# Linear attention in one kernel with routed experts: chunks of 128 tokens become pairs of 64-token chunks

## The chip, the cores and the metric

The kernel runs on one core of a Trainium2 chip. The metric is the device time of one execution in microseconds (us); lower is better. Three executions of the kernel before gave 908.94, 910.54 and 915.1 us, median 910.54. A separate execution was profiled; the page shown later is of that one.

The engines of the core are TensorE (PE in the profile, its weight loads are PEld), VectorE (DVE), ScalarE (ACT), GpSimd (POOL) and SyncE (SP, which only issues DMAs here). TensorE multiplies a stationary operand with a moving one and writes to PSUM, eight banks of 512 fp32 words for each of 128 partitions. GpSimd does not read PSUM in this kernel.

## The reference, cut

Four sequences of 2048 tokens with 256 features. Attention is linear, with 16 heads of 16 features and a running state; then each token goes to two of eight experts.

```python
mod = (_silu(c) @ wmod).reshape(4, 6, 1, -1)       # sa, ca, ga, sb, cb, gb
h = layernorm(x) * (1 + ca) + sa
# attention, w_qkv and w_out, phi = elu + 1:
q, k, v = phi(h @ wq.T), phi(h @ wk.T), h @ wv.T    # per head
S_t = S_{t-1} + k_t v_t^T ;  z_t = z_{t-1} + k_t    # over the tokens of a sequence
out_t = (S_t^T q_t) / max(z_t . q_t, 1e-6)
x = x + ga * (out @ w_out.T)
# experts:
h = layernorm(x) * (1 + cb) + sb
gates = softmax(h @ w_router.T); the best two, capacity 1280 rows for each expert
hidden = silu(h @ w_gate.T)
y = sum over the kept experts e of gate_e * (hidden @ w_down[e].T)
x = x + gb * y
```

## The kernel before

**Tiling.** The 8192 tokens are 16 groups `g` of 512 (`G`), four groups for each sequence (`GPB`). A group has four steps `j` of 128 tokens (`P`). The main loop runs over the 64 steps `s` (and one more), and in each it works on several groups at once: attention of group `g`; projections (`project`, `values`, `keys_by_token`), running key sums and denominators (`running_keys`, `denominators`, `scaled_q`, `heads_apart`) of `nxt` = g+1; normalisation of g+2; second normalisation and router of `prv` = g-1; positions and row stores of `old` = g-2 and g-3. After the 64 steps the experts run over the rows that were stored by expert (`gate`, `down`); that stage is not touched by the change.

**Order.** The order on TensorE, ScalarE, VectorE and GpSimd is the order in which the program is written (`manual_schedule`); each engine runs its list in that order, and the framework only adds the waits. Two accesses to one PSUM bank of one tile are kept apart by a wait, also where they touch different columns.

**Attention of one step.** The 256 features lie on partitions in two halves `h`; within a half, four strips of 32 partitions `a` hold two heads each, and `qeo` holds the scaled queries once for the even and once for the odd heads (`q`).

- `scores` (L494): 8 products, 32 features x 128 keys against 2 x 128 queries, into the four banks `psc`, one for each strip. Then `at` (L500): two VectorE instructions of 128x1024 that multiply the scores by the triangle `tri`.
- `attend` (L570), one step later: 16 products, 128 keys x 32 value columns (`vpad`) against 128 columns of `at`, into `po`.
- `keep_state` (L514): 8 products of the keys by token (`kk`) with the values, into other columns of `po`.
- `take_out`: one ScalarE copy of `po` (`both`, L525), then two GpSimd instructions: `s_acc` adds the step's sum (L538), `s_msk` leaves the blocks of single heads (L540).
- `from_state` (L557): 8 products of the state before the step with the queries, into the next `po`. The state it uses (`s_old`) was made in the step before.
- `project_out` (L588): two products `pw`, then VectorE adds them to `x` (L589) and takes statistics (L325).

An fp32 product appears in the trace as two matmul records.

**PSUM.** Three banks rotate for everything called `bank(...)` (projections, transposes, `pd` of `denominators`, `pw`, the router's `pl`, `lt` and `pp`), four are `psc` (also `pr` of `scaled_q`), one is `po`.

**Around it.** In step 0 stand the query projections `pq` (L375) and `deviations`; in step 1 `positions(old)` (`pp`, L707), the values `pv` (L397) and `shift_rows(old)` (L618, VectorE, 128x1024); in step 2 `denominators`, `to_features`, `scaled_q` (L471) and `dispatch(old)` (L731 to L753, some fifteen small VectorE instructions, two of them `sel`, L751); in step 3 the key projections `pk` of g+2, the router's `logits` and `ranks(prv)` (L669 to L690). `scale_rows` (L612) is a GpSimd multiplication of 128x1024. `send` issues indirect DMAs on GpSimd (L770), eight for each group: three in step 3, three in the next step 1, two in step 2.

## Time and profile before

| | us |
|---|---|
| median of 3 executions | 910.54 |
| profiled execution | 915.75 |
| its span, first to last instruction | 913.8 |
| PE busy | 823.0 |
| DVE busy | 568.2 |
| POOL busy | 477.1 |
| ACT busy | 419.0 |
| mean granted TensorE clock | 0.960 |

| stretch of the span, us | PE busy | DVE busy | POOL busy | clock |
|---|---|---|---|---|
| 0 to 72, start | 58.80 | 40.39 | 19.73 | 1.00 |
| 437.6 to 470.7, one group | 30.67 | 28.95 | 23.23 | 1.00 |
| 548 to 608, last group's routing | 28.00 | 29.59 | 33.48 | 0.75 |
| 608 to 872, experts | 263.96 | 87.29 | 106.37 | 0.99 |

Busy time is the time in which at least one instruction of the engine runs. A row of the order in time gives start, duration, engine, line, operation, output and inputs, the number of instructions merged, and in brackets the idle time of the engine before it and what released it. Durations of matmul records overlap, and their ends are modelled; the distance from one row's start to the next one's is the better measure of what a stage costs. The chain of work that ended last is given as start, duration, engine, line.

### The profile page before, as it was taken

The page shows a single profiled execution, that of the slowest core. Times are in us where ns is not written, and L with a number is a line of the kernel's source. Part 1 is how long each engine was busy: PE and PEld are TensorE (multiplying, and loading weights), DVE is VectorE, ACT ScalarE, POOL GpSimd, SP SyncE. Part 2 cuts the span into 40 slices and gives each one's busy share as a digit, 9 for nine tenths or more (in the row PEclk, how much of TensorE's full clock was granted, in tenths as well). Part 3 has the DMA queues.
Part 4 walks back from the last instruction along what each step waited for, and adds up shares of the span by engine and source line. Part 5 has one row for each costly group of instructions (what it writes and reads, how often), then busy time and mean ns, then how long its engine had stood idle before and what let it go on. Part 6 is the DMA issues. An engine that isn't in the chain of part 4 may idle for free.

```text
span 913.8 us, 20612 instructions
## 1 busy us (share of the span) xinstructions
PE 823.0 (90%) x8245; PEld 576.5 (63%) x8245; DVE 568.2 (62%) x1158; ACT 419.0 (46%) x972; POOL 477.1 (52%) x605
## 2 busy tenths in 40 slices
PE   6899979999999899999999976539999999999995
PEld 4477657567567567567667555326776767767764
DVE  3667768988888888888988886513333333333331
ACT  4557656656567567566566423212222222222220
POOL 2323446575586586576676586523443444434434
PEclk9999989999999999999999989659999999999998
DMA  8499851331442242432121111255665656545233
GB/s 307 135 358 347 188 110 72 124 136 66 129 136 68 105 136 69 120 111 77 61 76 55 49 49 39 66 200 134 148 138 106 134 112 145 110 100 112 35 34 41
DMA packets 75111, 108.25 MB, mean 118 GB/s; under 512 B 9578, under 2 KB 47218, under 8 KB 75016
## 3 DMA queue, kind: packets, MB, share of 16 engines
q1 hardware_dynamic: 47672, 68.91, 24.8%
q0 software_dynamic: 21760, 31.99, 16.3%
q10 hardware_dynamic: 5584, 6.04, 2.0%
q8 instruction: 65, 1.06, 0.5%
q14 instruction: 30, 0.25, 0.1%
HBM read 45.07 MB, written 74.69 MB: 131 GB/s over the span
## 4 chain that ended last, share of the span: by engine, by line
PE 66%; DVE 15%; issue 6%; POOL 5%; ACT 4%; DMA 2%; POOLq 0%; DVEq 0%; ACTq 0%; SPq 0%
PE ph L821 14%; PE pe L834 13%; PE pq L375 6%; PE pv L397 5%; PE psc L494 5%; PE pk L375 5%; PE po L570 5%; PE pw L588 4%; DVE at L500 3%; PE po L557 3%; DVE sel L751 2%; DVE qs L471 2%; POOL slots L770 2%; PE pte L810 2%; POOL out_dram L843 1%
## 5 line engine op out<-in xcount | busy, mean ns | idle before, releaser
L843 POOL DMA_INDIRECT out_dram<-y,tok x80 | 123.3, 1542 | 180.7 <-DVE y L839 126.2
L500 DVE TENSOR_TENSOR at<-psc,tri 128x1024 f32<-128x1024 f32 x128 | 150.1, 1214 | 29.2 <-PE psc L494 28.8
L770 POOL DMA_INDIRECT slots<-hrow,idx x128 | 129.4, 1011 | 52.5 <-issue 36.4
L821 PE MATMUL ph<-hTe,wg_sb 128*128 128x512 f32 (+1 forms) x384 | 153.5, 527 | 0.0
L834 PE MATMUL pe<-wd,hid 128*128 128x256 f32 x640 | 150.5, 379 | 0.0
L827 DVE SCALAR_TENSOR_TENSOR hid<-th,ph 128x512 f32<-128x512 f32 (+1 forms) x96 | 57.5, 599 | 146.3 <-ACT th L826 146.3
L834 PEld LDWEIGHTS pe<-wd,hid 128*128 128x128 f32 x640 | 121.6, 190 | 37.0 <-issue 23.0
L826 ACT ACTIVATE th<-ph 128x512 f32<-128x512 f32 (+1 forms) x96 | 50.5, 526 | 156.4 <-PE ph L821 156.4
L821 PEld LDWEIGHTS ph<-hTe,wg_sb 128*128 128x128 f32 x384 | 70.4, 193 | 39.0 <-issue 32.5
L375 PE MATMUL pk<-hTa,wqkv_sb 128*128 128x512 f32 x128 | 69.3, 671 | 22.6 <-DVE gates L671 22.6
L494 PE MATMUL psc<-qeo,k 32*128 32x256 f32 x1024 | 74.7, 405 | 2.4 <-DVE qs L471 1.0
L588 PE MATMUL pw<-wob,both 128*128 128x256 f32 x236 | 63.2, 391 | 7.8 <-ACT both L525 5.5
L570 PE MATMUL po<-at,vpad 128*32 128x128 f32 x2048 | 69.8, 278 | 0.0
L839 DVE SCALAR_TENSOR_TENSOR y<-pe,rows 128x256 f32<-128x256 f32 x80 | 38.7, 484 | 49.6 <-PE pe L834 49.6
L570 PEld LDWEIGHTS po<-at,vpad 128*32 128x32 f32 x2048 | 53.9, 111 | 17.1 <-issue 16.9
L375 PE MATMUL pq<-hTa,wqkv_sb 128*128 128x512 f32 x128 | 61.3, 604 | 0.0
L494 PEld LDWEIGHTS psc<-qeo,k 32*128 32x128 f32 x1024 | 47.8, 188 | 19.7 <-issue 13.3
L397 PE MATMUL pv<-wqkv_sb,hTa 128*128 128x256 f32 x256 | 59.2, 384 | 0.0
L588 PEld LDWEIGHTS pw<-wob,both 128*128 128x128 f32 x236 | 41.9, 192 | 25.1 <-issue 10.1
L813 ACT COPY hTe<-pte 128x512 f32<-128x512 f32 (+1 forms) x48 | 24.7, 514 | 70.8 <-PE pte L810 70.6
L375 PEld LDWEIGHTS pk<-hTa,wqkv_sb 128*128 128x128 f32 x128 | 23.5, 201 | 46.7 <-issue 44.9
L397 PEld LDWEIGHTS pv<-wqkv_sb,hTa 128*128 128x128 f32 x256 | 47.6, 190 | 6.5 <-issue 0.4
(166 smaller groups left out, 1348.3 us busy)
## 6 DMA issues: line engine op xcount, KB each, us to landing
slots<-free SPq DMA_DIRECT2D x80, 262.0 KB, 5.1
rows<-slots SPq DMA_DIRECT2D x16, 1048.0 KB, 6.1
x<-in_x_dram SPq DMA_DIRECT2D x16, 512.0 KB, 6.1
out_dram<-x SPq DMA_DIRECT2D x16, 512.0 KB, 2.9
hrow<-mod_d SPq DMA_DIRECT2D x48, 128.0 KB, 3.5
rows<-slots SPq DMA_DIRECT2D x8, 524.0 KB, 7.6
wd<-in_wdT_dram ACTq DMA_DIRECT2D x8, 512.0 KB, 4.6
slots<-hrow,idx POOLq DMA_INDIRECT x128, 2.9
```

The lines of the kernel that those rows point to most:

```text
L375: nc.tensor.matmul(pq, wqkv_sb[:, k, o + h * P : o + (h + 1) * P], hT[:, k, :], start=(k == 0), stop=(k == NH - 1))
L397: nc.tensor.matmul(pv[:, i * D : (i + 1) * D], hT[:, k, (j + i) * P : (j + i + 1) * P], wqkv_sb[:, k, 2 * D : 3 * D], start=(k == 0), stop ...
L494: nc.tensor.matmul(psc[:, a, h], kT[r : r + 32, h, cols], qeo[r : r + 32, h, :, cols], start=True, stop=True,)
L500: masked = nc.vector.tensor_tensor(at, psc[:, 2 * m : 2 * m + 2].rearrange("p i h q t -> p (i h q) t"), tri.unsqueeze(1).to_broadcast([P, ...
L570: nc.tensor.matmul(po[32 * a : 32 * a + 32, h * P : (h + 1) * P], vp[:, j, h * 4 + a, q : q + 2, :], att[a // 2][:, a % 2, h, q, :], start ...
L588: nc.tensor.matmul(pw[:, :D], oT[:, h, :], wob[:, h, :], start=(h == 0), stop=(h == NH - 1))
L770: row = nc.gpsimd.indirect_dma_start(out=slots[:, :], out_offset=bass.IndirectOffsetOnAxis(ap=idx[:, c, j : j + 1], axis=0), in_=hr[:, j0 ...
L821: nc.tensor.matmul(ph[:, :m], wg_sb[:, k, f * P : (f + 1) * P], hTs[b][:, k, :m], start=(k == 0), stop=(k == NH - 1),)
L826: nc.scalar.activation(th[:, :m], ph[:, :m], AF.Tanh, scale=0.5)
L827: nc.vector.scalar_tensor_tensor(hids[b][:, f, :m], th[:, :m], 1.0, ph[:, :m], ALU.add, ALU.mult)
L834: nc.tensor.matmul(pe[:, :D], hids[b][:, f, j * P : (j + 1) * P], wds[e][:, f, :], start=(f == 0), stop=(f == NF - 1),)
L843: put = nc.gpsimd.indirect_dma_start(out=out[:, :], out_offset=bass.IndirectOffsetOnAxis(ap=toks[b][:, j : j + 1], axis=0), in_=y, in_offs ...
```

## The change

Attention runs in chunks of 64 tokens (`C`), two chunks of one step side by side: the first on the lower half of the partitions or rows, the second on the upper half.

- `scores`: 16 products of 64 keys x 2 x 64 queries; the two chunks write the two halves of the partitions. Only the two diagonal 64x64 blocks of a step are computed, so the mask `at` is one instruction of 128x1024 with the triangle `tri_c`.
- `attend`: 32 products over 64 keys. `keep_state`: 16 products, a sum for each chunk.
- `take_out`: ScalarE copies the outcome (`oT`); VectorE masks the two sums out of PSUM (`new`); GpSimd adds them to the state one after the other (`st`).
- `from_state`: 16 products; the first chunk takes the state before the step, the second the state after the first chunk (`mid`), which is made in the same step.
- PSUM: two rotating banks instead of three, four of `psc`, two of `po`. `pw`, `lt` and `pd` now lie in free columns of `psc`; `pl` and `pp` in free columns of `po`.
- Order: `shift_rows(old)` moves from step 1 to step 0, `dispatch(old)` from step 2 to the end of step 1, `positions(old)` ahead of `take_out` of step 1, `logits` behind `keep_state`; the eight `send`s of a group are issued three in step 2, three in step 3 and two in the next step 1.

```diff
-    ps = ctx.enter_context(tc.tile_pool(name="ps", bufs=3, space=PSUM))
+    ps = ctx.enter_context(tc.tile_pool(name="ps", bufs=2, space=PSUM))
+    def score_banks(name):
+        G_["free"] = ps_sc.tile([P, 4, 512], F32, tag="psc", name=name)
+        return G_["free"]
...
+        for c in range(2):
+            nc.gpsimd.tensor_copy(tri_c[c * C : (c + 1) * C, :], tri[c * C : (c + 1) * C, c * C : (c + 1) * C])
...
     def denominators(g):
-        pd = bank(f"pd_{g}")
+        pr = G_["pr", g] = score_banks(f"pr_{g}")
+        pd = pr[:, 1, 2 * P : 3 * P]
...
     def scores(g, j):
+        psc = score_banks(f"psc_{g}_{j}")
+        hq = psc[:, :, : NH * 2 * C].rearrange("p a (h q t) -> p a h q t", h=NH, q=2)
+        for h in range(NH):
+            for c in range(2):
+                cols = slice(j * P + c * C, j * P + (c + 1) * C)
+                for a in range(4):
+                    r = 32 * a
+                    nc.tensor.matmul(
+                        hq[c * C : (c + 1) * C, a, h], kT[r : r + 32, h, cols], qeo[r : r + 32, h, :, cols],
+                        start=True, stop=True,
+                    )
+        at = w4.tile([P, 4, NH * 2, C], F32, tag="at", name=f"at_{g}_{j}")
+        masked = nc.vector.tensor_tensor(
+            at,
+            psc[:, :, : NH * 2 * C].rearrange("p a (n t) -> p a n t", t=C),
+            tri_c.unsqueeze(1).unsqueeze(1).to_broadcast([P, 4, NH * 2, C]),
+            ALU.mult,
+        )
...
+    def keep_state(g, j, cs):
+        for h in range(NH):
             for a in range(4):
+                for c in cs:
+                    rows_ = slice(c * C, (c + 1) * C)
+                    o = NH * C + h * 32
+                    nc.tensor.matmul(
+                        po[32 * a : 32 * a + 32, c, o : o + 32],
+                        G_["kk", g][rows_, j, h, 32 * a : 32 * a + 32], vp[rows_, j, h * 4 + a, 0::2, :],
+                        start=True, stop=True,
+                    )
...
+    def take_out(last, g, j, cs):
+            oT = G_[("oT",) + last] = w2.tile([P, NH, 2, C], F32, tag="oT", name=f"oT_{g}_{j}")
+            nc.scalar.copy(
+                oT.rearrange("p h c t -> p c h t"), po[:, :, :o].rearrange("p c (h t) -> p c h t", t=C)
+            )
...
+        nc.vector.tensor_tensor(
+            new[:, :k].rearrange("p c (h q e) -> p c h q e", h=NH, q=2),
+            po[:, :k, o : o + n].rearrange("p c (h q e) -> p c h q e", h=NH, q=2),
+            bd.unsqueeze(1).unsqueeze(1).to_broadcast([P, k, NH, 2, DH]), ALU.mult,
+        )
+        if not first:
+            nc.gpsimd.tensor_tensor(st[:, 0], G_["state"], new[:, 0], ALU.add)
+        if k == 2:
+            nc.gpsimd.tensor_tensor(st[:, 1], st[:, 0], new[:, 1], ALU.add)
+        G_["mid"] = st[:, 0]
+        G_["next"] = st[:, 1]
...
     def from_state(g, j):
+        for h in range(NH):
+            for c in cs:
+                st = G_["state"] if c == 0 else G_["mid"]
+                for a in range(4):
...
+                        po[r, c, h * C : (h + 1) * C], st[r, h * 32 : (h + 1) * 32],
+                        G_["qs", g][r, h, j * P + c * C : j * P + (c + 1) * C],
+        G_["state"] = G_["next"]
...
     def attend(g, j):
+                    for c in range(2):
+                        rows_ = slice(c * C, (c + 1) * C)
+                        nc.tensor.matmul(
+                            po[32 * a : 32 * a + 32, c, h * C : (h + 1) * C],
+                            vp[rows_, j, h * 4 + a, q : q + 2, :],
+                            att[rows_, a, h, q, :],
...
     def project_out(g, j):
-        pw = bank(f"pw_{g}_{j}")
+        pw = G_["free"][:, 0, 2 * P :]
...
-        pl = bank(f"pl_{g}_{j0}")
+        pl = G_["po"][:, 0, O_SMALL : O_SMALL + P] if beside else bank(f"pl_{g}_{j0}")
-        lt = G_["lt", part] = bank(f"lt_{g}_{j0}")
+        lt = G_["lt", part] = G_["free"][:, 1, 2 * P : 3 * P]
-        pp = bank(f"pp_{g}_{j0}")
+        pp = G_["po"][:, 0, O_SMALL : O_SMALL + P] if beside else bank(f"pp_{g}_{j0}")
...
+            keep_state(g, j, cs)
+            if prv is not None and j == (2 if early else 3):
+                logits(prv, beside=True)
+            if old is not None and j == 1:
+                positions(old, beside=True)
+            take_out(last, g, j, cs)
...
-            if old is not None and j == 3 and not early:
-                send(old, 0, 3)
+            if old is not None and j in (2, 3) and not early:
+                send(old, 3 * (j - 2), 3 * (j - 1))
...
             elif j == 0:
                     running_keys(nxt, (0,))
+                if old is not None:
+                    shift_rows(old)
             elif j == 1:
                 done()
-                if old is not None:
-                    positions(old)
                     running_keys(nxt, (1,))
                 if g >= 3:
-                    send((g - 3, 0, NT), 3, 6)
+                    send((g - 3, 0, NT), 6, 8)
...
-                if old is not None:
-                    shift_rows(old)
+                if old is not None:
                     dispatch(old)
             elif j == 2:
-                if g >= 3:
-                    send((g - 3, 0, NT), 6, 8)
...
-                elif old is not None:
-                    dispatch(old)
```

## The prediction

> **What bounds the kernel now.** I read the page's busy times first, then the busy time by stage, then the chain of work that ended last, and last the order in time of TensorE and VectorE inside one steady group. A group is 512 tokens in four steps of 128; a step is called step 0 to step 3.
>
> ```profile
> PE 823.0 (90%) x8245; PEld 576.5 (63%) x8245; DVE 568.2 (62%) x1158; ACT 419.0 (46%) x972; POOL 477.1 (52%) x605
> ```
>
> ```profile
> 370.00:404.60 34.60, 32.54 (x447) 22.32 (x446) 28.93 (x58) 21.66 (x54) 22.12 (x32) 0.95 0.31 98
> 404.60:437.60 33.00, 31.00 (x432) 21.63 (x430) 28.81 (x58) 21.77 (x54) 21.42 (x30) 1.00 0.27 92
> ```
>
> These two rows are two groups: time, then busy PE, PEld, DVE, ACT, POOL, then the granted clock. TensorE is busy 31.0 of 33.0 us and VectorE 28.8, so neither has room; the share of 62% on the page hides that, because VectorE idles through the expert stage (608 to 872 us), which the change does not touch. Four of the eleven groups between 133.6 and 503.8 us have the clock 0.95 and about 34.6 us, the others about 33.0; the mean is 33.65.
>
> The chain gives what attention costs TensorE in one step:
>
> ```profile
> 409.32 0.57 PE po L557 x16
> 409.89 1.07 PE psc L494 x16
> 410.96 1.01 PE po L570 x32
> 411.98 0.12 PE po L514 x16
> 412.10 1.91 PE pq L375 x4
> ```
>
> From state, scores, attend, keep state: 2.78 us, with two records to each product. A record of 512 columns alone takes 430 ns (the second projection half, 1.72 us for 4), so one of 256 would take 215; scores' 16 would take 3.4 us in a row and take 1.07, four rounds of four. So products on separate parts of the array overlap, over three-fold where four parts are in use, in all three shapes that the trace has.
>
> Where the group waits is seen in time, TensorE first, then VectorE and GpSimd:
>
> ```profile
> 420.24 1.03 PE L588 MATMUL pw<-wob,both 128*128 128x256 f32 x4
> 421.46 3.70 PE L397 MATMUL pv<-wqkv_sb,hTa 128*128 128x256 f32 x16
> 425.66 1.15 PE L494 MATMUL psc<-qeo,k 32*128 32x256 f32 x16
> 432.93 1.15 PE L494 MATMUL psc<-qeo,k 32*128 32x256 f32 x16
> 440.37 1.96 PE L375 MATMUL pk<-hTa,wqkv_sb 128*128 128x512 f32 x4 [1.96 <-DVE gates L671]
> 442.83 1.15 PE L494 MATMUL psc<-qeo,k 32*128 32x256 f32 x16
> ```
>
> ```profile
> 417.75 0.69 DVE L384 SCALAR_TENSOR_TENSOR q<-exq,q 128x512 f32<-128x512 f32 x1 [0.77 <-ACT q L380]
> 418.36 1.22 DVE L433 TENSOR_TENSOR_SCAN zc<-ones_g,k 128x512 f32<-128x512 f32 x1
> 419.49 2.33 DVE L500 TENSOR_TENSOR at<-psc,tri 128x1024 f32<-128x1024 f32 x2
> 424.22 1.27 DVE L618 TENSOR_TENSOR hrow<-hrow,modr 128x1024 f32<-128x1024 f32 x1
> 435.02 2.02 DVE L751 SCALAR_TENSOR_TENSOR sel<-rank,slot 128x32 f32<-128x32 f32 x1
> 437.56 2.35 DVE L500 TENSOR_TENSOR at<-psc,tri 128x1024 f32<-128x1024 f32 x2
> ```
>
> ```profile
> 434.63 2.36 POOL L612 TENSOR_TENSOR hrow<-hrow,modr 128x1024 f32<-128x1024 f32 x1
> ```
>
> The one long wait of TensorE is in step 3: `dispatch` keeps VectorE until 437.5, so the mask (scores were done at 434.0), the routing and with it a free bank for `pk` come late, 1.96 us. Inside `dispatch`, `sel` takes 2.02 instead of 0.18 because GpSimd's `scale_rows` holds it off until 436.99. In step 1 TensorE does not wait at all: `pw` at 420.24 runs in a bank of its own while VectorE is still on the mask.
>
> **The change, part by part.** I count from O = 416.52, where the second query projection is issued and step 0's state products start; the next such point is 449.53, 33.0 us on.
>
> *Products.* Records per step go from 16+16+32+16 = 80 to 32+32+64+32 = 160, with half the columns each (keep state: the same 32 columns, half the rows). From state uses the same four parts of the array twice, so it stays at 0.57. Scores and attend can now use eight parts. Slow end, by the attend row at today's overlap: 64 records at half of 28 ns are 0.9, scores 1.07, keep state 0.24, drains as now: 2.9 us. Fast end, eight side by side: scores 0.65 (half of the 0.86 of its four rounds, and 0.2 of filling and switching), attend 0.45, keep state 32 at the 7.5 ns of its row, 0.24, with a drain 0.8 together: 2.02 us. I take the fast end, since the trace shows overlap to follow the number of separate parts; 0.75 us per step then leave TensorE.
>
> A page of the Trainium skill speaks against it: "TensorE: Matmul & The Clock Gate", section "Wait — 56ns, not 53.3ns?", has matmuls start no less than about 25 ns apart, which would make 160 records an estimated 4.0 us a step. Here the 16 records in 0.12 us are 7.5 ns apart, so the row decides. The same page, "Measured speedup vs the span model", reports 10.6-fold overlap for sixteen tiles; no row here shows more than four parts at once.
>
> *Mask.* L500 falls from two instructions of 1.21 to one; one new product of 128x128 from PSUM (`new`) is priced by `den` L451, 128x128 from PSUM, 0.28. VectorE: 4 x (1.21 - 0.28) = 3.7 us less of its 28.8. ScalarE's copy loses 64 columns (0.42 to 0.37, the 256-column row) and GpSimd keeps two additions of about 0.32. None of these sits on the path by itself.
>
> *Banks.* `pw`, `lt` and `pd` now lie in the banks of the scores, behind the same step's mask: TensorE must wait for `at` before `pw`, for `gates` before step 3's `pw`, and the next scores must wait for VectorE's `x` addition. This is where the time is decided. `pp` and `pl` go into the outcome bank and only put a 0.19 copy ahead of another on ScalarE. With two banks left for the rest, each projection needs the evacuation two before it; the ScalarE copies stand 1 us or more ahead at every such place (`kk` by O+5.1, `pv` at O+6.4), so nothing; without that cover it is up to 0.75, one copy.
>
> *Moves.* `shift_rows` (1.27) goes from behind step 1's work to step 0, directly ahead of step 1's mask. `dispatch` goes from step 2 to step 1, ahead of step 2's mask. GpSimd's eight row stores per group (each 0.98 and 0.30 of gap) are issued a step earlier, 3, 3, 2; `scale_rows` stands behind three of them instead of two, 1.3 us later, and its user is now in the next step 0, over 10 us on. SP's queue is passed by nothing.
>
> *State.* The second half of from state needs the sum of the same step: keep state, ScalarE copy 0.37, `new` 0.28, GpSimd 0.32 (1.24 where VectorE holds it off, 423.17). In step 1 it stands behind `rstd` 1.68 and `qs` 1.27 and is ready by O+7.9 to 8.8; TensorE comes at O+9.9. Covered; if not, each microsecond late is 12 over the kernel.
>
> **The path of a group, summed.** Step 1: `q` ends at O+1.92 as now, scan O+3.06, `shift_rows` O+4.3, the mask O+5.5. TensorE reaches `pw` at about O+3.4 and waits 2.1 us. Then `pw` 0.86, `pv` 3.54, from state 0.57: step 2's scores at O+10.5 (now 9.14). VectorE meanwhile: `x` and its statistics to O+7.3, scan (1.22 to 1.77) O+8.6 to 9.1, `dispatch`: 432.70 to 437.65 is 4.95, without the blocked 1.84 it is 3.1, and GpSimd's `qs` now beside it can block up to 1.1. Ends at O+11.7 to 13.3; mask O+12.9 to 14.5. `pd` waits for it. Then `pd` 0.55, transposes 1.02, `pw` 0.86, `x` 0.5, `pr` 0.75 (its bank waits for `x`), transposes 1.02, state 0.6 and handovers: 5.4 us to step 3's scores, O+18.3 to 19.9 (now 16.4). Step 3: scores, attend, keep 1.45, `pl` 0.46, `pk` 1.96, `lt` 0.11; then routing 3.7 (439.82 to 443.5) and `x` 0.41 with handovers before the next scores: 8.25 (now 9.9; the wait for `dispatch` is gone, the wait for `x` behind the routing is new). Step 0: 6.0 (now 6.70). Together 32.6 to 34.2 us, middle 33.35, against 33.0. The 3 us that leave TensorE come back as waits of 2.1, about 1.9, 0.6 and 0.9.
>
> *Clock.* Four groups of eleven, with one idle stretch of some 1.9 us each, lost 1.6 to a half-speed spell. Two such stretches per group make 2 x 4/11 x 1.6 = 1.15 on average (0.58 now). The same page, section "HAM oscillation — how this bites in real kernels", asks only for idle gaps under about 3.4 us; by it these stretches are free and a group costs 33.35. The rows show 1.9 to be enough, so they decide.
>
> So a group takes 34.5 instead of 33.65, and twelve of them (2 to 13) cost +10.2. Groups 0 and 1, without `dispatch`, gain 3 us of products and lose them to the same waits: +0.5. From 510 us on, two masks stand on the chain (529.74, 547.74) and are 1.1 shorter each, with some handovers: -3. Sum +7.7 on the profiled execution of 915.75 us (span 913.8, 2 around it). That execution lies above the median of 910.54, so the forecast is 910.5 + 7.7 = **918 us**, its own range 907 to 929 from the ends of the path (-9, +10 over twelve groups).
>
> **Rivals.** *Eight parts do not overlap more than four* (slow end): 0.87 us more in steps 3 and 0, +21, less some 3 because shorter waits slow the clock less often: 936. For it: no row shows more than four. Against: overlap followed the parts in every shape.
>
> *The masks are ready in time* (the other side). If `qs` does not block `dispatch`, the scan stays at 1.22 and the clock spells stay as they are, a group is 32.6 + 0.58, -0.47: -5.6 - 2.5 makes 902; without any spell 896. It decides where step 2's mask ends before O+12.9. For it: VectorE has 3.7 us less to do. Against: the order puts `shift_rows` and `dispatch` directly ahead of the masks that TensorE now needs.
>
> *Records cost their issue, not their columns.* If 28 ns of the attend row stay at 64 columns, a step is some 4.2 us, 4.3 more per group than the forecast: 970. The 7.5 ns row speaks against it. That the change does less than it says I put at nothing: the program has the 160 records and the one mask per step.
>
> **How the numbers follow.** Forecast 0.57, four parts 0.14, masks in time 0.25, issue 0.04. A measurement here tells about 1% from no change, 9 us. Faster than 901.4 needs the second rival with fewer spells, or the forecast's path shorter than its ends: 0.19. Slower than 919.6: nearly half of the forecast's range and two rivals: 0.48. Between: 0.33. The range goes from 899, the second rival with fewer spells, to 938, the first.
>
> **What would show it.** Right: `at` x64, 1.2 us; scores to keep state in 2.0 us a step; TensorE idle before `pw` of step 1 for 2 us, released by the mask, and before `pd`; no wait of `pk` for `gates`; clock under 1.00 in most groups. Wrong: step 1's `pw` not waiting, or the four product stages at 2.8 us or above, or a group under 33 us.

## The result, and the profile after

The changed kernel takes 978.18 us (median of 4; 976.95 to 983.78) against 911.87 us for the kernel before: 1.0738 times as long, 95% interval 1.068 to 1.0796. Forecast were 918 us and a range up to 938. The profiled execution took 979.24 us, its span 977.5, against 913.8 before.

The page's busy times and its instruction queue (packets, MB, share), then the busy time by stage for two steady groups (time; busy PE, PEld, DVE, ACT, POOL; clock, DMA share, GB/s):

```profile
PE 820.3 (84%) x13365; PEld 578.4 (59%) x13365; DVE 497.5 (51%) x1158; ACT 410.3 (42%) x971; POOL 471.8 (48%) x611
...
q8 instruction: 105, 1.72, 0.7%
```

```profile
433.91:471.03 37.12, 31.24 (x767) 21.82 (x765) 24.06 (x56) 21.06 (x53) 22.05 (x32) 0.95 0.23 73
471.03:508.04 37.01, 30.55 (x735) 21.62 (x733) 24.11 (x56) 21.05 (x53) 23.71 (x32) 0.97 0.25 78
```

VectorE has lost 4.7 us of work a group (28.8 to 24.1; forecast was 3.7). But a group takes 37 us instead of 33.0 to 34.6. TensorE's records have gone from 8245 to 13365, and the queue that brings instructions from 65 packets to 105.

The order in time of TensorE, in the group that begins at O = 427.46:

```profile
427.46 0.65 PE L578 MATMUL po<-qs,st 32*32 32x64 f32 x32
428.04 0.69 PE L510 MATMUL psc<-qeo,k 32*64 32x128 f32 x32
428.66 0.80 PE L594 MATMUL po<-at,vpad 64*32 64x64 f32 x60
...
432.97 1.10 PE L611 MATMUL psc<-wob,oT 128*128 128x256 f32 x4 [1.72 <-DVE at L515]
...
441.26 0.64 PE L460 MATMUL pr<-qs,hpick 128*32 128x128 f32 x16 [1.23 <-DVE at L515]
...
456.83 0.70 PE L510 MATMUL psc<-qeo,k 32*64 32x128 f32 x32 [1.88 <-DVE x L612]
...
458.55 3.58 PE L388 MATMUL pq<-hTa,wqkv_sb 128*128 128x512 f32 x4
```

The products are short, and the two waits for the mask are there, ahead of `pw` (432.97) and of `pd` (441.26, printed under the name of its bank, `pr`). New is a third wait, 1.88 us ahead of step 0's scores. Behind it the next projection takes 3.58 us instead of 1.9: the granted clock there is 0.50. VectorE and ScalarE show where it comes from:

```profile
451.22 0.19 DVE L694 TENSOR_TENSOR gates<-psc,mx 128x32 f32<-128x32 f32 x1
453.33 0.19 DVE L697 TENSOR_REDUCE sm<-gates 128x4 f32<-128x32 f32 x1 [1.93 <-ACT gates L695]
```

```profile
450.88 0.60 ACT L392 ACTIVATE exk<-pk 128x512 f32<-128x512 f32 x1
451.38 0.59 ACT L393 ACTIVATE k<-pk 128x512 f32<-128x512 f32 x1
451.85 1.33 ACT L498 ACTIVATE qeo<-qs,par 128x512 f32<-128x512 f32 x2
453.08 0.22 ACT L695 ACTIVATE gates<-gates 128x32 f32<-128x32 f32 x1
```

The router's exponent (L695) could run at 451.4, when VectorE has its argument. It stands on ScalarE behind an evacuation and `heads_apart` and runs at 453.08. The order on ScalarE is that of the kernel before; there `dispatch` made the argument late, and ScalarE had been idle for 0.49 us when it came:

```profile
440.26 0.23 ACT L672 ACTIVATE gates<-gates 128x32 f32<-128x32 f32 x1 [0.49 <-DVE gates L671]
```

The second new thing is a kind of idle time that the trace puts down to nothing it shows ("issue"):

```profile
99.48 0.25 PE L532 MATMUL po<-vpad,kk 64*32 64x32 f32 x4 [2.19 <-issue]
129.30 0.59 PE L611 MATMUL psc<-wob,oT 128*128 128x256 f32 x1 [5.58 <-issue]
302.30 1.02 PE L388 MATMUL pk<-hTa,wqkv_sb 128*128 128x512 f32 x2 [2.56 <-issue]
```

Thirteen such stops sum to 22.4 us; the kernel before has one, 3.6 us at 122.5. Its row, and its instruction queue on the page:

```profile
122.51 1.72 PE L361 MATMUL pta<-ident,xna 128*128 128x128 f32 x7 [3.63 <-issue]
...
q8 instruction: 65, 1.06, 0.5%
```

I numbered TensorE's instructions in the trace (weight loads, matmuls, semaphore events) in order of their start: the first instruction behind each of the thirteen, and behind the one before the change, has the same number, 193, modulo 256. The changed kernel's 105 packets carry 1.72 MB, 16.4 KB each. So these are the places where TensorE's own program comes in blocks of 256 instructions, and the 5120 added records, two instructions each, are the 40 added blocks.

Where 63.7 us of span went, from the start of `values` of one group to that of another:

| stretch (before / after, us) | before | after | difference | stops in it |
|---|---|---|---|---|
| start to 81.1 / 84.0 | 81.1 | 84.0 | +2.9 | 0 / 0.9 |
| two groups, DMA engines 0.86 / 0.80 busy in the first | 69.3 | 86.6 | +17.3 | 3.6 / 11.3 |
| eleven groups, to 522.2 / 580.8 | 371.8 | 410.2 | +38.4 | 0 / 8.4 |
| last routing, to 608.9 / 672.2 | 86.7 | 91.4 | +4.7 | 0 / 1.8 |
| experts, to the end | 304.9 | 305.3 | +0.4 | |

### The profile page after: what moved, and what is told of

Same layout as the page of the kernel before. It is cut to its first block, busy times and chain, and to the rows that moved or that the text cites. A ratio compares the mean times of both kernels' runs of the same rounds, so it can differ in the third digit from the quotient of the medians.

```text
span 977.5 us, 30896 instructions
## 1 busy us (share of the span) xinstructions
PE 820.3 (84%) x13365; PEld 578.4 (59%) x13365; DVE 497.5 (51%) x1158; ACT 410.3 (42%) x971; POOL 471.8 (48%) x611
## 3 DMA queue, kind: packets, MB, share of 16 engines
q8 instruction: 105, 1.72, 0.7%
## 4 chain that ended last, share of the span: by engine, by line
PE 64%; DVE 12%; ACT 9%; issue 8%; POOL 3%; DMA 2%; POOLq 0%; DVEq 0%; ACTq 0%; SPq 0%
PE ph L844 13%; PE pe L857 12%; PE pq L388 6%; PE pk L388 6%; PE psc L611 5%; DVE at L515 3%; PE po L594 3%; PE psc L510 3%; PE pv L410 3%; ACT xna L322 2%; PE pte L833 2%; PE pta L374 2%; PE ptm L374 2%; DVE zc L446 1%; PE po L578 1%
## 5 line engine op out<-in xcount | busy, mean ns | idle before, releaser
L611 PE MATMUL psc<-wob,oT 128*128 128x256 f32 x196 | 57.5, 418 | 43.4 <-DVE at L515 22.7
L515 DVE TENSOR_TENSOR at<-psc,tri_c 128x1024 f32<-128x1024 f32 x64 | 78.0, 1218 | 25.7 <-PE psc L510 25.5
L611 PEld LDWEIGHTS psc<-wob,oT 128*128 128x128 f32 x196 | 37.0, 203 | 58.7 <-issue 26.9
L388 PE MATMUL pq<-hTa,wqkv_sb 128*128 128x512 f32 x128 | 69.2, 670 | 0.0
L510 PE MATMUL psc<-qeo,k 32*64 32x128 f32 x2048 | 45.5, 283 | 26.0 <-ACT xna L295 14.8
L559 POOL TENSOR_TENSOR st<-st,new 128x64 f32<-128x64 f32 x60 | 28.8, 480 | 74.1 <-DVE new L553 73.9
L410 PEld LDWEIGHTS pv<-wqkv_sb,hTa 128*128 128x128 f32 x256 | 53.0, 207 | 14.8 <-issue 6.2
L594 PE MATMUL po<-at,vpad 64*32 64x64 f32 x4096 | 57.5, 232 | 0.9 <-issue 0.9
L418 ACT COPY vpad<-pv 128x256 f32<-128x256 f32 x64 | 20.7, 375 | 82.5 <-PE pv L410 82.5
L836 ACT COPY hTe<-pte 128x512 f32<-128x512 f32 (+1 forms) x48 | 24.7, 514 | 71.1 <-PE pte L833 71.0
L594 PEld LDWEIGHTS po<-at,vpad 64*32 64x32 f32 x4096 | 46.2, 108 | 12.6 <-issue 12.4
```

The lines of the kernel that those rows point to most:

```text
L388: nc.tensor.matmul(pq, wqkv_sb[:, k, o + h * P : o + (h + 1) * P], hT[:, k, :], start=(k == 0), stop=(k == NH - 1))
L410: nc.tensor.matmul(pv[:, i * D : (i + 1) * D], hT[:, k, (j + i) * P : (j + i + 1) * P], wqkv_sb[:, k, 2 * D : 3 * D], start=(k == 0), stop ...
L510: nc.tensor.matmul(hq[c * C : (c + 1) * C, a, h], kT[r : r + 32, h, cols], qeo[r : r + 32, h, :, cols], start=True, stop=True,)
L515: masked = nc.vector.tensor_tensor(at, psc[:, :, : NH * 2 * C].rearrange("p a (n t) -> p a n t", t=C), tri_c.unsqueeze(1).unsqueeze(1).to_ ...
L594: nc.tensor.matmul(po[32 * a : 32 * a + 32, c, h * C : (h + 1) * C], vp[rows_, j, h * 4 + a, q : q + 2, :], att[rows_, a, h, q, :], start= ...
L611: nc.tensor.matmul(pw, oT[:, h].rearrange("p c t -> p (c t)"), wob[:, h, :], start=(h == 0), stop=(h == NH - 1))
```

## Experiments

The runs fell on several chips of two kinds: on one kind the kernel before takes 911 to 914 us, on the other 956 to 963 us. Every ratio is against the kernel before on the same chip. What the expectations call the first and the second chip are these two kinds.

**The exponent first, and the moves undone.** `exp_first` issues the router's transposition, maximum and exponent ahead of `heads_apart` and the key projection; `order_back` leaves the changed order on ScalarE and puts `shift_rows`, `dispatch` and the row stores back where they were.

```diff
# exp_first, step 3
+                if prv is not None and not early:
+                    weights(prv)      # lt, mx, gates: the first half of ranks
                 heads_apart(nxt, (0,))
                 project(nrm, "k", 0, D, 2, later=True)
                 heads_apart(nxt, (1,))
-                logits_by_token(prv)
                 ranks(prv)
# order_back
-  step 0: shift_rows(old)   step 1: dispatch(old)   send 3, 3, 2 in steps 2, 3, 1
+  step 1: shift_rows(old)   step 2: dispatch(old)   send 3, 3, 2 in steps 3, 1, 2
```

> The changed kernel with the routing's transposition, maximum and exponent (lt, mx, gates) ahead of heads_apart and the first key projection in step 3, the rest of the routing where it was. Theory A: in the changed kernel VectorE waits 1.93 us for the exponent (453.33 behind ScalarE's exk, k and qeo), and TensorE then 1.87 us for x before step 0's scores. With the exponent before them the routing ends 2 to 3 us earlier, that last wait goes, and with it the half-clock spell that follows: 1.9 to 2.5 us for each of eleven groups, 950 to 958 us. Rival B (the bound is VectorE's and TensorE's work in that step, not the order on ScalarE): the wait moves to the earlier lt, nothing or under 6 us: 972 to 980 us.

> The changed kernel with the moves undone: shift_rows back in step 1, dispatch back in step 2, the row stores back at three in step 3, three in step 1, two in step 2. Theory A (the loss sits in three places: TensorE's own instruction stream stops at block boundaries, 22.5 us against 3.6; the routing's exponent in step 3 stands on ScalarE behind an evacuation, some 2 us a group; half-clock spells): the moves are not the cause. Step 1's pw then waits 1.2 us less (shift_rows 1.20 gone from ahead of the mask) and pd some 1.2 less, but dispatch (3.1 to 5 us) comes back ahead of step 3's mask and of the routing, so that step 3 gets longer by 2 to 4 us: between 975 and 995 us. Rival B (the moves put VectorE work ahead of the masks that TensorE now needs, and that is the loss): 1.7 and 1.2 us of waits go, with their spells, some 4 us a group on twelve groups: 930 us or less.

`exp_first`: 946.59 us, 1.0424 (1.0348 to 1.0499); again on another chip 948.7, 1.0363. That is 31.6 us less than the changed kernel, more than expected. The two steadiest groups, then TensorE around the place of the third wait, then VectorE:

```profile
378.61:411.77 33.16, 29.33 (x766) 21.16 (x765) 24.18 (x56) 20.93 (x53) 21.92 (x32) 1.00 0.32 106
411.77:444.88 33.11, 29.32 (x767) 21.15 (x766) 24.12 (x56) 20.94 (x53) 21.87 (x32) 1.00 0.25 82
```

```profile
427.18 0.33 PE L676 MATMUL psc<-ident,lgT 128*128 128x128 f32 x1 [0.39 <-ACT lgT L668]
...
432.32 0.69 PE L510 MATMUL psc<-qeo,k 32*64 32x128 f32 x32
...
433.99 1.99 PE L388 MATMUL pq<-hTa,wqkv_sb 128*128 128x512 f32 x4
```

```profile
428.34 0.19 DVE L711 TENSOR_REDUCE sm<-gates 128x4 f32<-128x32 f32 x1 [0.29 <-ACT gates L695]
```

The exponent takes 0.29 us out of VectorE's chain instead of 1.93, the scores of step 0 wait for nothing, and the projection runs at full clock. In the changed kernel the twelve waits there were 22.3 us and those of step 3's `pw` 7.4; `lt`, now early, gives 5.4 back. The rest of the gain, some 7 us, fits the clock, but no run shows it apart: ten of eleven groups were below 1.00, here seven, and the mean clock of the execution was 0.940, here 0.952. Against the kernel before, the profiled execution is still 27.8 us longer, 14.4 of them in the two early groups and 9.2 in the eleven; its stops at blocks are 24.7 us instead of 3.6, so most of what is left may be stops.

`order_back`: 963.06 us, 1.057 (1.0508 to 1.0632): between the two expectations, both missed. With `dispatch` in step 2 VectorE comes late to the router (`lt` waits 1.87 us for the mask) and its wait for the exponent is 0.29 us. So the moves did what they were to do, and in doing it laid bare the order on ScalarE. A third thing is needed: in the kernel before with the same moves (`before_moved` below) VectorE waits as long for the exponent,

```profile
440.26 0.18 DVE L674 TENSOR_REDUCE sm<-gates 128x4 f32<-128x32 f32 x1 [1.93 <-ACT gates L672]
```

and step 0's scores (440.96) wait for nothing, because `pw` has a bank of its own there and the scores need not wait for `x`. The moves, the order on ScalarE and `pw` in the scores' banks make the third wait together.

**Records or time.** Two versions of the kernel before with about the same added TensorE time, one in 80 records a step, one in four.

```diff
# more_records, keep_state
-        for h in range(NH):
+        for h in [h for _ in range(6) for h in range(NH)]:
# more_columns, end of keep_state
+        for _ in range(2):
+            nc.tensor.matmul(both[:, D + 64 : D + 256], G_["kk", g][:, j, 0, :], wqkv_sb[:, 0, :192], start=True, stop=True)
```

> The kernel before, with the products of keep_state issued six times over: 80 more matmul records in each of the 60 steps that keep the state, as many as the change adds, at 7.5 ns each 0.6 us a step, 36 us in all if TensorE's path takes all of it. Refill theory: each record is two instructions, so the program grows by 9600 instructions, 37 blocks of 256, and TensorE stops at some of the block boundaries as the changed kernel does: 910 + 36 + 8 to 19 us of stops, 954 to 966 us, and the trace shows stops named issue that sum to over 10 us. Rival (the stops of the changed kernel come from something else in it): 940 to 948 us, and stops of no more than some 4 us, as in the kernel before.

> The kernel before with two unused products of 128x192 columns added to each keep_state: four records a step of together about 0.64 us, the same busy time as the 80 small ones, but only 480 instructions in all. Both theories: 910 + up to 38, 940 to 950 us, with stops named issue of no more than some 4 us. Under the refill theory it is 8 to 19 us faster than the kernel with more records; under the rival the two differ by less than 5 us.

957.32 us, 1.05 (1.0446 to 1.0554), as the theory expected, against 937.97, 1.0286 (1.0233 to 1.034), 2 us under its range: 19.4 us between them. The page and the order in time of the first, and the one stop of the second:

```profile
q8 instruction: 102, 1.67, 0.7%
```

```profile
102.36 0.71 PE L464 MATMUL pr<-rden,spread 32*128 32x128 f32 x12 [3.24 <-issue]
110.20 0.80 PE L514 MATMUL po<-vpad,kk 128*32 128x32 f32 x70 [1.23 <-issue]
119.43 0.74 PE L570 MATMUL po<-at,vpad 128*32 128x128 f32 x18 [1.62 <-issue]
129.00 0.64 PE L557 MATMUL po<-qs,s_msk 32*32 32x128 f32 x16 [2.36 <-issue]
```

```profile
128.79 0.42 PE L574 MATMUL po<-at,vpad 128*32 128x128 f32 x8 [1.71 <-issue]
```

Nine stops, again all at number 193 of 256, 10.1 us against 1.7. The three early groups take 11.0 us more, the eleven groups behind them 7.5. Of those 7.5 only 1.1 are stops: the 96 small records take 1.33 us (425.13 to 426.46), the 16 with the two wide products 1.08, so the added work isn't quite equal, and only 8.4 of the 19.4 us are stops. So records alone bring stops at the blocks, about half of the changed kernel's; its other half needs more than their number.

`few_records` goes the other way: the kernel with the early exponent, attend and keep_state replaced by nine products with 18 records that don't compute their outcome.

```diff
# few_records
-        (64 records of attend)
+        for c, i in ((0, 0), (0, 1), (1, 0)):
+            nc.tensor.matmul(po[:, c, :P], G_["kk", g][:, j, c, :], att[:, 2 * c + i]..., ...)
-        (32 records of keep_state)
+        for c in cs * 3:
+            nc.tensor.matmul(po[:, c, o : o + 64], G_["kk", g][:, j, c, :], vp[:, j, :2, 0::2, :], ...)
```

> The kernel with the early exponent (1.036 to 1.042 times the kernel before, 24.7 to 27.1 us of stops at instruction blocks), with attend and keep_state left out and replaced by a few products of whole partitions that read the same tiles and keep the banks and the waits: three of 128x128 and six of 128x64, some 1.0 us a step as the 96 records had, but 18 records. The outcome of attention and the state are thereby not computed. 82 records a step, as many as the kernel before. Refill theory: the program is about 65 blocks long instead of 105, the stops fall to under 5 us and with them some of the half-clock spells that follow them: 1.010 to 1.022. Rival (the stops belong to the way these groups wait, or to the DMA load, not to the length of the program): stops of 15 us or more, 1.032 to 1.045.

66 packets, and one stop at a block, of 0.27 us, where the early exponent had 24.7 us of them. The three early groups, 122.2 us in a kernel with 105 blocks on a chip of the same kind (`spread_init` below), take 109.3. The time, 993.17 us, 1.0299, says nothing: the replacements took 2.2 us a step, not 1.0. So the stops follow the length of the program; what they are worth in all isn't measured by this run.

**The banks.** Waits taken out one by one from the kernel with the early exponent: `pw` in a rotating bank, then `pd` too, then `dispatch` at the end of step 3 (row stores three in step 0, three in step 1, two in step 2).

```diff
# pw_bank
-        pw = G_["free"][:, 0, 2 * P :]
+        pw = bank(f"pw_{g}_{j}")[:, :D]
# pw_pd_bank, late_dispatch: also
-        pd = pr[:, 1, 2 * P : 3 * P]
+        pd = bank(f"pd_{g}")[:, :P]
```

> The kernel with the early exponent (946.6 us, group 33.15 us), and pw of project_out back in one of the two rotating banks instead of the free columns of the scores' banks. Bank theory (what TensorE gained in products it waits for again, because pw sits behind the same step's mask): the 1.7 us wait ahead of step 1's pw goes; pv's second half then waits some 0.4 us for the x addition, and VectorE reaches dispatch 1.1 us earlier, so that the wait of pd stays at 1.2 to 1.5: a group of 31.8 to 32.2 us, 930 to 937 us. Rival (VectorE's chain of scan, shift_rows, mask, x and dispatch sets step 1 and 2, and the wait only changes its place to pd): a group of 32.9 to 33.2 us, 943 to 949 us.

> As the kernel before in this list, and pd of denominators in a rotating bank too. Bank theory: the wait of pd for step 2's mask (1.2 us) goes, but den still stands behind dispatch and that mask on VectorE, and the second transposition pta needs the bank that den frees: 0.3 to 0.6 us of wait stay there. A group of 31.0 to 31.5 us, 921 to 929 us. Rival (VectorE's chain sets it): no more than 3 us below the kernel with pw alone.

> As the kernel with pw and pd in rotating banks, and dispatch moved behind the key projections at the end of step 3, where the mask behind it has a whole step to spare; the row stores then go out three in the next step 0, three in step 1, two in step 2. If the order of VectorE's work was the rest of the loss, the waits of step 1 and 2 go to under 0.6 us each and step 0 stays free of waits: a group of 29.5 to 30.7 us, 905 to 918 us, near the kernel before in spite of 20 us of stops at instruction blocks. Rival (dispatch only displaces its wait to the next scores or to the query evacuation): a group of 31 us or more, 920 us or more.

On a chip of the second kind: 999.21 us (1.0365), 1002.89 (1.0388), 1041.6 (1.0804). The expected times were meant for the first kind, so only the ratios compare: none of the three gains came, and the rivals aren't contradicted. Two were repeated beside the early exponent on a chip of the first kind:

> The kernel with the early exponent once more, so that it stands beside the next two on one chip. On the first chip it took 1.042 times the time of the kernel before. Both theories: 1.035 to 1.05 times again.

> pw back in a rotating bank, once more, beside the kernel with the early exponent on one chip. On the second chip it took 1.0365 times the time of the kernel before, where 1.020 to 1.027 was expected. Bank theory: 1.0 to 1.5% under the kernel with the early exponent (the 1.7 us wait ahead of step 1's pw on twelve groups, less what comes back at pd and pv). Rival (the wait only changes its place): within 0.4% of it.

> pw and pd in rotating banks and dispatch at the end of step 3, once more on this chip. On the second chip it took 1.080 times the time of the kernel before, with 79 gaps of together 44 us inside small products, in the steps where its row stores are issued. Theory: without such gaps its groups take 29.5 to 31 us and it is 2 to 4% under the kernel with the early exponent; with them it is 3 to 5% over it. Rival (the order of dispatch itself is worse, through VectorE): 2% or more over it with no such gaps in the trace.

948.7 us (1.0363, 1.0304 to 1.0423), 968.08 (1.0611, 1.0546 to 1.0675) and 954.7 (1.0452, 1.0413 to 1.0491). `pw` in a rotating bank is 2% worse and `late_dispatch` 0.6%, outside all that was expected of either. The trace of TensorE with `pw` in a bank shows the wait moving:

```profile
441.52 0.64 PE L460 MATMUL pr<-qs,hpick 128*32 128x128 f32 x16 [1.95 <-DVE at L515]
442.10 1.40 PE L374 MATMUL pta<-ident,xna 128*128 128x128 f32 x8
443.62 2.08 PE L611 MATMUL pw<-wob,oT 128*128 128x256 f32 x4
...
460.17 1.88 PE L388 MATMUL pq<-hTa,wqkv_sb 128*128 128x512 f32 x4 [1.70 <-DVE new L553]
```

The 1.72 us ahead of `pw` are gone, but `pd` now waits 1.95 instead of 1.2 with a half-clock spell behind it (`pw` 2.08 instead of 1.03). The 1.70 us ahead of `pq` are something else: the profile names VectorE, but the weight load before it had started at 458.40, and `pq` has number 193 of 256, as at the same wait of the group before (1.93 us at 422.84). Both are stops at blocks, like the 3.18 us at 384.12; in the other groups nothing waits there. New in all groups is that the second halves of the projections wait 0.3 to 0.5 us for ScalarE. The eleven groups' clock is 0.95 instead of 0.97. `late_dispatch` has no wait of `pw` or `pd` for the mask and the clock at 0.99, but its steadiest groups take 33.4 to 33.9 us: with every small result in two rotating banks, five handovers of 0.24 to 0.66 us each stand on the path, and in most other groups step 2's `pw` waits 1.39 us for a copy (`hTa`). In these orders, with two banks for the rest, a wait that was taken out came back in other places.

`shift_early` keeps `pw` where it is, moves `shift_rows` to the start of step 0, where VectorE idles, and takes only `pd` out.

```diff
# shift_early, step 0
+                    shift_rows(old)
                 project(nxt, "q", 0, 0, 1)
 ...
-                    shift_rows(old)
```

> The kernel with the early exponent, with shift_rows at the beginning of step 0 (where VectorE idles some 2 us for the query's evacuation) instead of its end, and pd in a rotating bank, so that it doesn't wait for step 2's mask. If single waits can still be taken out while pw stays in the scores' bank: pw's wait in step 1 falls from 1.7 to 0.5 us and pd's from 1.2 to nothing, with some 0.7 back at the second transposition: a group of 31.5 to 32.2 us, 1.022 to 1.030. Rival (as with pw in a rotating bank, a wait that is taken out comes back at the next one on VectorE's chain, with a half-clock spell behind it): 1.036 to 1.050.

971.89 us, 1.008 (1.0052 to 1.0109), on a chip of the second kind: the best of the versions in chunks of 64 by its ratio, below what was expected. But the kernel before is itself slowed on that chip (below), so the ratio isn't to be set beside 1.036; beside `spread_init` (1.0298, below), the nearest run on the same kind, it is 2% lower. Its groups take 35.8 us there, not the 31.5 to 32.2 of the theory.

`spread_init` spreads the writes that fill the slots over twelve steps, for the stops:

> The kernel with the early exponent, with the 48 writes that fill the slots in steps 0 to 5 spread over steps 0 to 11, four instead of eight for each step. In that kernel the DMA engines are busy 0.95 to 1.00 from 50 to 130 us, and the stops at instruction blocks there sum to 10.8 of 24.7 us, up to 4.37 us each; later ones, at a share of 0.2 to 0.3, are mostly 0.3 to 2.6. If the blocks come late because the same DMA engines are full, the stops before 135 us fall to under 6 us and the time by 4 to 8 us, 938 to 943 us. Rival (a block comes late because records use up instructions faster than any refill, whatever else moves): the stops stay at 9 to 12 us there and the time within 3 us of 946.6.

993.52 us, 1.0298; the stops before 135 us sum to 12.7 us, the longest 7.9, although the DMA engines' share fell to 0.78 (50 to 90 us) and 0.56 (90 to 130). The stops did not fall, as the rival says, and are a little above its 9 to 12 us; why the early ones are the longest stays open.

**The moves on the kernel before.**

```diff
# before_moved: shift_rows to the end of step 0, dispatch to the end of step 1, send 3, 3, 2 in steps 2, 3, 1
# before_late:  dispatch behind finish_keys in step 3, send 3, 3, 2 in steps 0, 1, 2
```

> The kernel before with nothing but the change's moves: shift_rows at the end of step 0, dispatch at the end of step 1, the row stores three in step 2, three in step 3 and two in the next step 1. It tells what the moves do alone. Theory: pk's wait for the gates in step 3 (1.96 us) goes, but dispatch now stands ahead of step 2's mask and of den, and scaled_q's products wait some 2 us for rden: 0.99 to 1.01. Rival 1 (the moves are a gain that the new banks then take back): 0.975 to 0.985. Rival 2 (the moves are themselves a loss): 1.015 or more.

> The kernel before with dispatch at the end of step 3, behind finish_keys, and the row stores three in the next step 0, three in step 1, two in step 2; attention in chunks of 128 and three rotating banks as they were. If pk's wait of 1.96 us for the gates is what can still be had from a step: it goes, dispatch then lies ahead of step 0's mask, whose banks are needed only at step 1's scores, a group of 31.2 to 31.8 us instead of 33.0: 0.970 to 0.982, a version that beats both. Rival (dispatch in step 0 delays the query's evacuation and the scan, and the wait comes back there): 0.99 to 1.01.

On a chip of the second kind: 920.23 us, 0.9525 (0.9483 to 0.9568), and 976.04, 1.0121 (1.0069 to 1.0173). The first beat its best expectation, the second lies above all of its own: step 0's mask came late and the next scores waited for it, up to 3.9 us. So the moves were run again, with the kernel before traced beside them, and an earlier trace of it was taken on a chip of the first kind:

> The kernel before, unchanged, for its trace on the same chip as the next three. In the kernels with pw in a rotating bank and with the writes spread, on a chip where the kernel before took 962.6 us, the trace shows trains of gaps of 0.3 to 0.7 us between records inside the attention's small products, 38 to 79 of them between 180 and 560 us; the kernel with the early exponent, on the first chip, shows none. If the trains belong to that chip, this run has them too wherever it takes some 960 us (20 or more, 10 us or more), and has 5 or fewer where it takes some 910 us. If they belong to the kernels (pw in a rotating bank, spread writes), this run has 5 or fewer at either time.

> The kernel before, unchanged, for a trace beside the next run. On one chip the kernel before takes 911 to 914 us, on the other 963 us; the trace on the first shows no gaps of 0.25 to 0.9 us beside GpSimd's row stores. If this runs on the second chip and its 50 us come from there: 40 or more such gaps between 180 and 560 us, all within 1.6 us after a row store's start. If it runs on the first: fewer than 12, and some 912 us.

> The kernel before with nothing but the change's moves, once more. On the second chip it took 0.9525 times the kernel before, in groups of 33.7 us that hold some 1.2 us of gaps beside the row stores. Theory (the moves are a gain by themselves: pk's wait for the gates goes, and step 2's mask is not awaited while pw has a bank of its own): on the first chip a group of 32.4 to 32.9 us instead of 33.8, 0.980 to 0.990, 892 to 904 us; on the second 0.945 to 0.96 again. Rival (the gain belongs to the second chip alone, because the row stores come to lie beside other products): 0.995 to 1.005 on the first chip.

919.09 us, 0.9553 (0.9526 to 0.9581), with the kernel before at 955.93 in its trace. `pk` waits for the gates no longer (19.9 us in ten groups before, none with the moves). The other part of the gain lies in what the second kind of chip does to the kernel before (25 gaps beside row stores, where 40 or more were expected). Here are `pd`'s rows of the kernel before on the two kinds, with GpSimd's row stores of the second:

```profile
392.73 0.62 PE L446 MATMUL pd<-qs,hpick 128*32 128x128 f32 x16
```

```profile
411.41 0.38 PE L446 MATMUL pd<-qs,hpick 128*32 128x128 f32 x3
412.03 0.41 PE L446 MATMUL pd<-qs,hpick 128*32 128x128 f32 x4 [0.23 <-issue]
412.75 0.43 PE L446 MATMUL pd<-qs,hpick 128*32 128x128 f32 x6 [0.31 <-issue]
413.51 0.42 PE L446 MATMUL pd<-qs,hpick 128*32 128x128 f32 x3 [0.32 <-issue]
```

```profile
410.71 1.10 POOL L770 DMA_INDIRECT slots<-hrow,idx  x1 [0.17 <-issue]
412.11 0.97 POOL L770 DMA_INDIRECT slots<-hrow,idx  x1 [0.30 <-issue]
413.38 0.97 POOL L770 DMA_INDIRECT slots<-hrow,idx  x1 [0.30 <-issue]
```

From `pd` to step 3's scores the kernel before takes 5.16 us on the first kind (392.73 to 397.89) and 8.90 on the second (411.41 to 420.31), which is the whole difference of its groups there (33.0 and 36.7). With the moves `pd` is as slow on the second kind, but step 2 now waits for VectorE anyway (`dispatch`, mask, `den`), and a group takes 33.75 us. So the moved kernel beats both there. It was not run on the first kind, where the kernel before has groups of 33.3 and 33.8 us on average in two traces: how much of the 4.5% would stay is open, and the same 33.75 us would be no gain.

## Why the prediction was wrong, point by point

- **Products: right.** Eight parts of the array do run side by side: from state, scores, attend and keep state lie 2.25 us apart (427.46 to 429.71), forecast 2.02, before 2.78. The rival of four parts is out, and so is the one of records that cost 28 ns to issue: attend's 60 records start within 0.58 us, 9.7 ns apart. Its 970 us lay nearest to the result, but not for its reason.
- **Banks and order in steps 1 and 2: right.** `pw` starts at O+5.51 (forecast 5.5, wait 1.72 for 2.1), step 2's scores at O+10.57 (10.5), step 3's at O+19.15 (18.3 to 19.9). The rival with masks in time is out.
- **Step 3: the step that failed.** "Then routing 3.7" was taken over from a trace in which the exponent found ScalarE idle, and "the wait for `dispatch` is gone" named no successor. From step 3's scores to step 0's: 10.22 us, forecast 8.25; VectorE takes 5.28 us from `mx` to `x` (450.99 to 456.27) instead of 3.7, 1.93 of it idle for the exponent. The wait for `x` was named, the order on ScalarE behind it was not read. With the exponent early it is 7.85, and the group 33.11 to 33.16, forecast 33.35. The early exponent was worth 31.6 us.
- **A term that was missing: instruction blocks.** The records were priced by their time alone. Stops are 22.4 us instead of 3.6. The sign was on the page before: 65 packets in the instruction queue and a stop of 3.63 us "issue" that I read as nothing. The Trainium skill, "Runtime: NRT & Kernel Launch", section "Instruction fetch mechanics", gives TensorE's program as blocks of 256 instructions, 16 KiB, fetched ahead, and calls the cost of a boundary mostly hidden. The traces agree on the blocks (16.4 KB a packet, all stops at one number of 256) and not on the cost: 13 stops on 105 blocks, up to 5.58 us. `few_records` and `more_records` show that the stops come with the length of the program.
- **Clock: the term was too small.** Ten of eleven groups lie under 1.00, as "most" said; the mean clock of the eleven is 0.958 against 0.977 before, which is 1.6 us a group instead of the forecast 1.15. The third wait and the stops bring spells that two waits a group didn't count. So a group of 37.3 us, where 34.5 was forecast, misses by roughly 2.0 in step 3, 0.8 in stops and 0.4 in clock, less 0.4 elsewhere.
- **The edges.** The two early groups were to cost +0.5 and cost 17.3, of which stops are 7.7; the rest was not taken apart, but the first of them has the clock at 0.90, before 1.00. The last routing was to gain 3 and lost 4.7. Its clock is 0.71 against 0.79; no run tells more.

## What to carry to other kernels

When a wait is removed, read the queue of every engine that the freed chain passes through, in the new order, for what is issued ahead: a short instruction behind longer ones cost about as much here (31.6 us) as the products saved (0.53 us in each of 64 steps). Smaller and more numerous products have a second price beside their time, the program itself: count instructions, look for stops at equal numbers modulo the block and for the packets of the instruction queue, also in the kernel that one starts from. With a bank less, each result that has to lie somewhere else can bring a wait of its own; taking one out showed others in all the orders tried here. And a wait that the profile names after an engine can be a stop at a block: look at the number too.

## What the runs showed of the hardware that was not expected

- TensorE stops at number 193 of 256 of its instruction stream, for 0.6 to 5.6 us in the changed kernel and up to 8.2 us in other versions, at some block boundaries and not at others. All over 4 us lie between 94 and 131 us, on both kinds of chips.
- On some chips TensorE's records come slowly while GpSimd issues indirect row stores, and only then: in the ten traces of that kind 377 of 382 gaps of 0.25 to 0.9 us inside attention's small products and `pd` (180 to 560 us) begin within 1.6 us of a store's start, which is a third of the time; in the ten traces on the other kind there are 21 such gaps in all, and 19 of them are stops at blocks. Projections of 512 columns beside such stores keep their 0.43 us a record. Which records meet the stores then decides some per cent, which is more than most of these changes. The cause stays open.
- The length of a wait alone doesn't tell whether a half-clock spell follows. In the changed kernel the wait of 1.88 us at 456.83 was followed by one, an equal one at 381.64 and the 1.72 us at 432.97 were not; in the kernel before, the 1.96 us at 440.37 was not. More is told by a grid: within one execution the spells start whole multiples of 3.41 us apart and last 3.41 us or a multiple (150 to 560 us). On that grid, in the changed kernel, all 7 stretches of full clock with over 1.86 us of idle TensorE were followed by a spell, 2 of 10 with 1.7 to 1.86 us, and none of 94 with less; in the kernel before 5 of 6, 1 of 4 and 0 of 103. So a wait of 1.9 us brought a spell where it fell nearly whole into one such stretch, and that is chance: the grid lay 0.46 us apart in two executions of the kernel before.
